# A residual image added to 128 channels: by matmul broadcast and two passes, or by DMA broadcast and one

## The chip, the cores and the metric

The kernel runs on one core of a Trainium2 chip. The metric is the device time of one execution in microseconds (us), so lower is better. The core has five engines that run side by side, each with its own queue of instructions, taken in order: PE (TensorE, matrix products, with PEld for its weight loads), DVE (VectorE), ACT (ScalarE), POOL (GpSimd) and SP (SyncE), which here issues nearly all transfers between DRAM and SBUF. Products land in PSUM[...]. Everything is float32.

## The reference, cut to what matters

Four layers follow each other on an image of 256 × 256 points with 128 channels. Only the last is touched. It normalises the image by groups of channels, runs two kinds of convolution with shifted residuals, and adds the result to its input:

```
def c1(t):  # 9 taps along W, 128 channels to one
    return conv(t, w1) + b1
def c2(t):  # centre tap alone: a 128 x 128 product for each point
    return einsum('bhwc,cd->bhwd', t, w2[0, 4]) + b2
t = relu(c1(x))
y = concat([x[:, :1], x[:, 1:] + t[:, :-1]], axis=1)
u = relu(c1(y))
z = u + roll(y, 1, axis=1)       # with its last rows rearranged
v = relu(c2(z))
p = concat([z[:, :, :1], z[:, :, 1:] + v[:, :, :-1]], axis=2)
r = relu(c2(p))
q = r + roll(p, 1, axis=2)       # with its last columns rearranged
x = x + q
```

Here the inner x is the normalised one, (x - m) * r. Since c1 yields one channel, t and u are images of one number for each point, the same for all channels. So z is the normalised x, shifted by one row, plus an image e that is the sum of u and the shifted t. With the norm written out, z = r3 * x + k0 + e, where r3 and k0 = -m * r3 are one number per channel.

## The kernel before, in words

Channels are the partitions. The stage works on slices of 8 image rows (R = 8, 2048 points, NR = 32 slices), in a loop over s from 0 to 33 (L1419), and on blocks of 16 rows (two slices) for the one-channel images. Within `tc.manual_schedule()` each engine takes its instructions in the order in which the code writes them, so the text of the loop sets the order of the work.

The images take a detour through DRAM. `taps` (L1221) multiplies a slice of x with the nine taps on PE and stores the sums in sD. `load_block` (L1251) reads a block's shifted taps back, with the image spread over 128 partitions; `sum_taps` (L1260), `image_u` (L1276) and `image_e` (L1287) form t, u and e on DVE. t goes through tD (`keep_t`, `load_t`), and e is stored in eD, rows of NP = 264 with margins. In the loop, slices with even s run `sum_taps` and `image_u` of a block at their end, and slices with odd s `image_e`.

e must then reach all 128 channels. `load_e` (L1298) reads the two slices of a block into four partition groups of a small tile `p9_er`, four DMAs a block. `broadcast_rows` (L855) spreads a slice over the partitions with four products of PE with a column of `sel`, into two PSUM tiles of the pool psX. `start_z` (L1307) has ACT write r3 * x + k0 into the tile `p9_z` (two pieces, of 1 and 7 rows), and `finish_z` (L1321) has DVE add the spread e from PSUM, in two halves.

From z on, `p_half` (L1337) takes half a slice: `product9` (L1328) forms w2c times z on PE, and DVE's pass at L1340 turns it into p, reading the product in PSUM and z in SBUF. A constant per channel, `kcol[:, 0:1]`, brings in the bias. `residual` (L1344) adds shifted p to q's start on POOL, reading two tiles in SBUF; q's start is x plus a constant, written by ACT (L1430). `q_half` (L1350) does for r what p_half does for v. The products of p and q share a PSUM pool psM of two buffers, so a product waits until DVE has read the one before the last.

In slice s the order is: on PE the product of z(s), the spread of e(s+1), the product of p(s-1), the taps of slice s+6, and the transposes of q(s-2); on DVE two passes for p(s), two for z(s+1), four for q(s-1) and the image's passes; on POOL the residual of s as soon as p(s) is complete; on SP the load of x(s+8), t or e of a block, the stores of taps, and the output of slice s-2.

`emit` (L1362) transposes q in 16 blocks of 128 points and stores the slice with point k * 128 + p in partition p, which makes a run of 512 bytes for each point.

Of the kernel before, what the change touches and what calls it, by code (L numbers as in the profile page):

```python
# [8 lines left out]
F32 = mybir.dt.float32  # L9
AF = mybir.ActivationFunctionType  # L10
ALU = mybir.AluOpType
# [4 lines left out]
P = 128  # L16
N = 256
D = 128
T = N * N
SC = 2048  # L20
NSC = T // SC
CK = 512
# [5 lines left out]
TAPS = 9  # L28
# [3 lines left out]
def kernel(ctx: ExitStack, tc: tile.TileContext, a: dict, out: bass.AP):  # L32
    nc = tc.nc
    x_tok = a["x"].rearrange("b i j d -> (b i j) d")
    out_tok = out.rearrange("b i j d -> (b i j) d")
# [26 lines left out]
    NP = N + 8  # L62
# [5 lines left out]
    eD = dram.tile([1, N * NP], F32, name="eD")  # L68
# [140 lines left out]
    with tc.tile_pool(name="x0", bufs=1) as xres, tc.tile_pool(name="p0", bufs=3) as sb:  # L209
# [18 lines left out]
        with tc.tile_pool(name="f0", bufs=1) as fsb, tc.tile_pool(name="f0ps", bufs=1, space=PSUM) as ps:  # L228
            cen = fsb.tile([P, P], F32, name="f0_c")
            nc.vector.tensor_scalar(cen, ident, -1.0 / D, None, ALU.add)  # L230
            wa = fsb.tile([P, 4 * D + NH], F32, name="f0_a")
            nc.vector.tensor_scalar(wa, w0, ln_w, None, ALU.mult)
            wb = fsb.tile([P, 4 * D + NH], F32, name="f0_b")
            nc.vector.tensor_scalar(wb, w0, ln_b, None, ALU.mult)
            for lo, hi in ((0, 4 * D), (4 * D, 4 * D + NH)):
                pc = ps.tile([P, hi - lo], F32, name="f0_pc", tag=f"f0_pc{lo}")
                nc.tensor.matmul(pc, lhsT=cen, rhs=wa[:, lo:hi], start=True, stop=True)
                nc.vector.tensor_copy(w0c[:, lo:hi], pc)
            pq = ps.tile([P, 3], F32, name="f0_pq")
            for j, i in enumerate((0, 1, 3)):  # L240
                nc.tensor.matmul(pq[:, j : j + 1], lhsT=w0[:, i * D : (i + 1) * D], rhs=ln_b, start=True, stop=True)
            nc.vector.tensor_copy(cqkg, pq)
            pv = ps.tile([P, D], F32, name="f0_pv")
            nc.tensor.matmul(pv, lhsT=ones, rhs=wb[:, 2 * D : 3 * D], start=True, stop=True)
            for k in range(4):
                nc.vector.tensor_copy(cv[:, k, :], pv)

            w2c_ = const.tile([P, 6, D], F32, name="w2c_")
            wa2 = fsb.tile([P, 6, D], F32, name="f0_a2")
            nc.vector.tensor_scalar(wa2[:, 0:5, :], w2[:, 0:5, :], lniw, None, ALU.mult)  # L250
            nc.vector.tensor_scalar(wa2[:, 5, :], w2[:, 5, :], lnow, None, ALU.mult)
            for lo, hi in ((0, 4), (4, 6)):
                pc = ps.tile([P, (hi - lo) * D], F32, name="f0_pc2", tag=f"f0_pc2{lo}")
                nc.tensor.matmul(
                    pc, lhsT=cen, rhs=wa2[:, lo:hi, :].rearrange("p w d -> p (w d)"), start=True, stop=True
                )
                nc.vector.tensor_copy(w2c_[:, lo:hi, :].rearrange("p w d -> p (w d)"), pc)
            pb2 = ps.tile([P, 6], F32, name="f0_pb2", tag="f0_pb2")
            for i in range(6):
                nc.tensor.matmul(  # L260
                    pb2[:, i : i + 1], lhsT=w2[:, i, :], rhs=lnib if i < 5 else lnob, start=True, stop=True
                )
            nc.vector.tensor_tensor(b2w, b2w, pb2, ALU.add)

            pb2 = ps.tile([P, TAPS + 1], F32, name="f0_ps", tag="f0_pb2")
            nc.tensor.matmul(pb2[:, :TAPS], lhsT=ones, rhs=w1[:, :TAPS], start=True, stop=True)
            nc.vector.tensor_copy(wsum, pb2[:, :TAPS])
            pk = pb2[:, TAPS : TAPS + 1]
            nc.tensor.matmul(pk, lhsT=w2c, rhs=b2, start=True, stop=True)
            nc.vector.tensor_scalar(kcol[:, 0:1], b2, -1.0, None, ALU.mult)  # L270
            nc.vector.scalar_tensor_tensor(kcol[:, 1:2], pk, -1.0, b2, ALU.mult, ALU.subtract)
            nc.vector.scalar_tensor_tensor(kcol[:, 2:3], b2, 2.0, pk, ALU.mult, ALU.add)
            pt_ = ps.tile([P, NH], F32, name="f0_pt")
            nc.tensor.matmul(pt_, lhsT=ones, rhs=wb[:, 4 * D :], start=True, stop=True)
            nc.vector.tensor_copy(ctri, pt_)
# [923 lines left out]

    R = 8
    NR = N // R
    H = R // 2
# [4 lines left out]
    with tc.tile_pool(name="p9", bufs=2) as sb, tc.tile_pool(name="p9psM", bufs=2, space=PSUM) as psM, tc.tile_pool(  # L1209
# [1 line left out]
    ) as psX, tc.manual_schedule():  # L1211
        x3r = x3T.rearrange("d (h w) -> d h w", w=N)
        xs, zs, pbs, qs, blocks = {}, {}, {}, {}, {}
        ers = [sb.tile([P, CK], F32, name=f"p9_er{i}", bufs=1) for i in range(2)]

        def load9(s):
            if s < NR:
# [77 lines left out]
                nc.sync.dma_start(image_rows(eD, N - 2, 1), e[P - 8 : P, :])  # L1295
                nc.sync.dma_start(image_rows(eD, N - 1, 1), k["t"][P - 8 : P, 4 : 4 + BW])

        def load_e(b):  # L1298

            e_chunks = eD.rearrange("o (s c h w) -> c (o s) h w", c=4, h=2, w=NP)  # L1300
            for c in range(4):
                nc.sync.dma_start(
                    ers[b % 2][32 * c : 32 * c + 2, :].rearrange("s (h w) -> s h w", h=2),
                    e_chunks[c, 2 * b : 2 * b + 2, :, 4 : 4 + N],
                )

        def start_z(s):  # L1307

            zs[s] = sb.tile([P, R, N], F32, name="p9_z", bufs=3)

            def take(lo, hi, src):
                nc.scalar.activation(zs[s][:, lo:hi, :], src, AF.Identity, bias=k0, scale=r3)

            take(0, 1, xs[s - 1][:, R - 1 : R, :] if s else xe[:, 1:2, :])
            if s + 1 < NR:
                take(1, R, xs[s][:, 0 : R - 1, :])
            else:
                take(1, R - 2, xs[s][:, 0 : R - 3, :])
                take(R - 2, R, xs[s][:, R - 2 : R, :])

        def finish_z(s):  # L1321
            eb = broadcast_rows(psX, ers[s // 2 % 2], s % 2, "p9_eb")
            zf = zs[s].rearrange("p h w -> p (h w)")
            for h in range(2):
                hs = slice(h * H2, (h + 1) * H2)
                nc.vector.tensor_tensor(zf[:, hs], eb[h], zf[:, hs], ALU.add)

        def product9(src, h):  # L1328
            pm = psM.tile([P, H, N], F32, name="p9_pm")
            for c in range(2):  # L1330
                r = h * H + 2 * c
                nc.tensor.matmul(  # L1332
                    pm[:, 2 * c : 2 * c + 2, :], lhsT=w2c, rhs=src[:, r : r + 2, :], start=True, stop=True
                )
            return pm

        def p_half(s, h):  # L1337
            rows_ = slice(h * H, (h + 1) * H)
            pm = product9(zs[s], h)
            nc.vector.scalar_tensor_tensor(  # L1340
                pbs[s][:, rows_, 1:N], pm[:, :, 0 : N - 1], kcol[:, 0:1], zs[s][:, rows_, 1:N], ALU.max, ALU.add
            )

        def residual(s):  # L1344
# [17 lines left out]
        def emit(s):  # L1362
            qf = qs.pop(s).rearrange("p h w -> p (h w)")
            ot = sb.tile([P, SC // P, D], F32, name="p9_o")
            for h in range(2):
                pt = psX.tile([P, 2 * H, D], F32, name="p9_pt", tag="x")
                for k in range(2 * H):
                    b = h * 2 * H + k
                    nc.tensor.transpose(pt[:, k, :], qf[:, b * P : (b + 1) * P], ident)  # L1369
                nc.scalar.copy(ot[:, h * 2 * H : (h + 1) * 2 * H, :], pt)  # L1370
            nc.sync.dma_start(
                out_tok[s * SC : (s + 1) * SC, :].rearrange("(k p) d -> p k d", p=P), ot
            )

        xe = sb.tile([P, 2, N], F32, name="p9_xe", bufs=1)
        nc.sync.dma_start(xe, x3r[:, N - 2 : N, :])
        for s in range(4):
            load9(s)
        for er in ers:
            nc.gpsimd.memset(er, 0.0)  # L1380
        S0 = sb.tile([P, TAPS, 2 * BW + 8], F32, name="p9_S")
        nc.vector.memset(S0, 0.0)

# [8 lines left out]
        taps(xe, N - 2, 1)  # L1392
        for s in range(2):
            taps(xs[s], s * R, 4)
        start_z(0)
        load_taps(S0, N - 1, 1, BW, BW + 4, P - 8)
        blocks[-1] = dict(St=S0)
        load_block(0)
# [3 lines left out]
        def image(b):  # L1402
            sum_taps(b)
            keep_t(b)
            load_t(b)
            image_u(b)
            image_e(b)
            load_e(b)

        image(0)  # L1410
        for s in range(2, 4):
            taps(xs[s], s * R, 4)
        for s in range(4, 6):
            load9(s)
        finish_z(0)
        load_block(1)
        for s in range(6, 8):
            load9(s)
        for s in range(NR + 2):  # L1419
            load9(s + 8)  # L1420
            b = s // 2 + 2
            if s % 2 == 1 and 2 < b < NB:
                load_t(b)
            if s % 2 == 0 and 3 < b <= NB:
                load_e(b - 1)
            if s < NR:
                pbs[s] = sb.tile([P, R, N], F32, name="p9_pb")
                nc.scalar.activation(pbs[s][:, :, 0:1], zs[s][:, :, 0:1], AF.Identity, bias=kcol[:, 0:1])
                qs[s] = sb.tile([P, R, N], F32, name="p9_q", bufs=3)
                nc.scalar.activation(qs[s], xs[s], AF.Identity, bias=kcol[:, 2:3])  # L1430
                if s + 1 < NR:
                    start_z(s + 1)
                p_half(s, 0)
                p_half(s, 1)
                del xs[s]
            if s + 1 < NR:
                finish_z(s + 1)
            if 0 < s <= NR:
                q_half(s - 1, 0)
                q_half(s - 1, 1)  # L1440
# [207 lines left out]
```

## Time and profile before

| | |
|---|---|
| time, median of 3 runs | 3525.54 us (3513.11 to 3529.35) |
| span of the profiled execution | 3502.3 us |
| last stage (layer 3), in that span | about 3078 to 3502 us |
| busy over the whole span | PE 89%, DVE 66%, ACT 56%, POOL 46% |
| DVE's p passes, L1340, 128x1020 | 64 of 1276 ns |
| DVE's z passes, L1326, 128x1024 | 64 of 1219 ns |
| DVE's q passes, L1354, 128x1016, and their tails, L1357 | 64 of 1270 and of 216 ns |
| POOL's residual, L1346, 128x2024 | 32 of 4505 ns |
| ACT's z pieces, L1312, from 3150 to 3450 us | 1874 and 594 ns |
| ACT's copies of the transposes, L1370, same stretch | 1016 ns |

A row of the profile's groups names a line of the code, the engine and the operation, the tiles (out<-in), the shape, how many there were and the mean time of one, and then how long the engine stood idle just before them and who released it. A timeline row gives start, duration, engine, line and tiles, and merges neighbours of one kind (x8). A float32 product of 512 columns stands as two records. The rows of stretches give, for each stretch, the busy time of every engine and the share of time that the DMA engines were moving packets.

### The profile page before, as it was taken

The page shows a single profiled execution, that of the slowest core. Times are in us where ns is not written, and L with a number is a line of the kernel's source. Part 1 is how long each engine was busy: PE and PEld are TensorE (multiplying, and loading weights), DVE is VectorE, ACT ScalarE, POOL GpSimd, SP SyncE. Part 2 cuts the span into 40 slices and gives each one's busy share as a digit, 9 for nine tenths or more (in the row PEclk, how much of TensorE's full clock was granted, in tenths as well). Part 3 has the DMA queues.
Part 4 walks back from the last instruction along what each step waited for, and adds up shares of the span by engine and source line. Part 5 has one row for each costly group of instructions (what it writes and reads, how often), then busy time and mean ns, then how long its engine had stood idle before and what let it go on. Part 6 is the DMA issues. An engine that isn't in the chain of part 4 may idle for free. (4 is left out here: it accounts for less than half of the span.)

```text
span 3502.3 us, 52445 instructions
## 1 busy us (share of the span) xinstructions
PE 3131.9 (89%) x20260; PEld 1652.7 (47%) x20260; DVE 2316.9 (66%) x2637; ACT 1962.3 (56%) x2198; POOL 1604.9 (46%) x821
## 2 busy tenths in 40 slices
PE   3576999999999999966597899999999999859998
PEld 3523555555555555521432344444899533314444
DVE  4624888888888888852398454544555677647776
ACT  3564777777777777733243454443444466535665
POOL 4002777777777777731487000000555354414443
PEclk7787999999999999989798999999999999979999
DMA  9983333333333333349599686865999798846764
GB/s 334 325 316 114 102 120 115 106 122 115 105 122 112 108 122 111 110 161 392 168 337 351 233 309 229 299 255 206 345 349 351 297 335 303 291 171 193 206 198 136
DMA packets 309867, 759.49 MB, mean 217 GB/s; under 512 B 77627, under 2 KB 148957, under 8 KB 259437
## 3 DMA queue, kind: packets, MB, share of 16 engines
q1 hardware_dynamic: 298749, 746.43, 60.5%
q0 software_dynamic: 10864, 9.65, 0.9%
q8 instruction: 162, 2.65, 0.3%
q14 instruction: 92, 0.75, 0.1%
HBM read 468.28 MB, written 287.66 MB: 216 GB/s over the span
## 5 line engine op out<-in xcount | busy, mean ns | idle before, releaser
L489 DVE TENSOR_TENSOR p_e<-p_S,triT 128x1024 f32<-128x1024 f32 x512 | 609.4, 1212 | 144.5 <-PE p_S L479 144.5
L499 POOL TENSOR_TENSOR p_es<-p_e 128x1024 f32<-128x1024 f32 x256 | 602.9, 2365 | 125.8 <-issue 67.5
L497 ACT ACTIVATE p_e<-p_e,mbT 128x1024 f32<-128x1024 f32 x512 | 551.8, 1137 | 61.4 <-DVE p_e L489 59.6
L946 PE MATMUL p_pm<-p_zn,wf 128*128 128x512 f32 x1040 | 450.4, 595 | 1.4 <-DVE p_zn L963 1.4
L464 PE MATMUL p_mm<-p_xn,wf 128*128 128x512 f32 x768 | 407.6, 614 | 9.3 <-POOL p_xn L437 9.3
L437 POOL TENSOR_TENSOR p_xn<-p_xn,p_rs 128x1024 f32<-128x1024 f32 x64 | 153.5, 2398 | 451.4 <-DMA p_x<-xT 260.4
L946 PEld LDWEIGHTS p_pm<-p_zn,wf 128*128 128x128 f32 x1040 | 197.7, 191 | 254.9 <-issue 248.1
L479 PE MATMUL p_S<-p_q,p_k 32*128 32x256 f32 x4096 | 295.4, 400 | 5.0 <-DVE p_e L489 5.0
L479 PEld LDWEIGHTS p_S<-p_q,p_k 32*128 32x128 f32 x4096 | 185.8, 184 | 161.5 <-PE p_mm L455 91.7
L1346 POOL TENSOR_TENSOR p_q<-p_q,p_pb 128x2024 f32<-128x2024 f32 x32 | 144.2, 4505 | 249.6 <-DVE p_pb L1340 249.6
L1606 PE MATMUL tp_z<-p_B,tp_at 128*128 128x256 f32 x1024 | 250.3, 387 | 2.1 <-DMA p_B<-bD 1.8
L512 PE MATMUL p_o<-p_e,p_v 128*32 128x256 f32 x4096 | 247.6, 382 | 0.0
L1011 POOL DMA_DIRECT2D rs__18021<-rs2D x4 | 2.1, 518 | 532.1 <-PE p_pm L946 532.1
L1054 POOL TENSOR_TENSOR k<-k,p_sq 128x512 f32<-128x512 f32 x128 | 162.9, 1273 | 135.2 <-ACT p_sq L1052 135.2
L1163 POOL TENSOR_TENSOR p_x<-p_x,p_g 128x2048 f32<-128x2048 f32 x30 | 136.2, 4540 | 177.8 <-DVE p_g L1150 146.9
L1606 PEld LDWEIGHTS tp_z<-p_B,tp_at 128*128 128x128 f32 x1024 | 185.3, 191 | 24.4 <-issue 2.2
L464 PEld LDWEIGHTS p_mm<-p_xn,wf 128*128 128x128 f32 x768 | 126.4, 191 | 114.1 <-issue 89.7
L1053 DVE TENSOR_TENSOR k<-tp_z,k 128x512 f32<-128x512 f32 x128 | 88.5, 691 | 128.5 <-ACT p_sq L1052 128.5
L512 PEld LDWEIGHTS p_o<-p_e,p_v 128*32 128x32 f32 x4096 | 120.0, 109 | 109.3 <-ACT p_g L470 41.5
L979 DVE SCALAR_TENSOR_TENSOR p_b<-p_pm,b2w,p_b 128x1024 f32<-128x1024 f32 x64 | 82.2, 1284 | 125.4 <-PE p_pm L946 111.0
L455 PEld LDWEIGHTS p_mm<-wf,p_xn 128*128 128x128 f32 x1024 | 135.3, 192 | 62.3 <-issue 61.1
L1050 ACT COPY p_K<-tp_z 128x512 f32<-128x512 f32 x128 | 75.1, 586 | 159.6 <-PE tp_z L1606 159.6
(353 smaller groups left out, 5902.5 us busy)
## 6 DMA issues: line engine op xcount, KB each, us to landing
p_x<-x2T SPq DMA_DIRECT2D x64, 1024.0 KB
p_x<-x1T SPq DMA_DIRECT2D x48, 1024.0 KB
p_x<-in_x_dram SPq DMA_DIRECT2D x32, 1024.0 KB
p_x<-xT SPq DMA_DIRECT2D x64, 512.0 KB
p_rs<-rsD SPq DMA_DIRECT2D x64, 512.0 KB
p_rb<-rzD SPq DMA_DIRECT2D x256, 128.0 KB
x1T<-p_x SPq DMA_DIRECT2D x64, 512.0 KB
aD<-p_a SPq DMA_DIRECT2D x32, 1024.0 KB
```

The source lines that it names most:

```text
L437: nc.gpsimd.tensor_tensor(xn, xn, t["rs"], ALU.mult)
L464: nc.tensor.matmul(pm, lhsT=w, rhs=t["xn"][:, cs_], start=True, stop=True)
L479: nc.tensor.matmul(Ss[h // 2][:, h % 2, u, :], lhsT=t["k"][hp, r * N + u * P : r * N + (u + 1) * P], rhs=t["q"][hp, r * N : (r + 1) * N], ...
L489: nc.vector.tensor_tensor(e[:, :, 2 * p : 2 * p + 2, :].rearrange("p u h n -> p h u n"), Ss[p], triT[:, 2 * p : 2 * p + 2, :, :], ALU.add,)
L497: nc.scalar.activation(e[:, u, :, :], e[:, u, :, :], AF.Exp, bias=mbT[:, u, i : i + 1])
L499: nc.gpsimd.tensor_tensor(es, e[:, 0, :, :], e[:, 1, :, :], ALU.add)
L512: nc.tensor.matmul(t["o"][hp, r % 2, :], lhsT=t["v"][:, r * 2 + u, hp], rhs=e[:, u, h, :], start=(u == 0), stop=(u == 1),)
L946: nc.tensor.matmul(pm[:, c, :], lhsT=wf2[:, i, :], rhs=zns[s][:, k * CK : (k + 1) * CK], start=True, stop=True)
L1054: nc.gpsimd.tensor_tensor(k2, k2, sq, ALU.add)
L1163: nc.gpsimd.tensor_tensor(xs7[s], xs7[s], gts[s], ALU.add)
L1346: nc.gpsimd.tensor_tensor(q[:, :, 1 : N - 2], q[:, :, 1 : N - 2], pb[:, :, 0 : N - 3], ALU.add)
L1606: nc.tensor.matmul(pz[:, t, :], lhsT=at[:, u, t * P : (t + 1) * P], rhs=Bc[:, u, :], start=(u == 0), stop=(u == 1))
```

## The change

Three things change in the last stage.

- e goes to the channels by DMA. `spread_e` reads a slice of eD, margins included, into every partition of z's own tile, which grows to rows of 264; `load_e`, `p9_er`, and PE's spread go away. It is issued two slices ahead of the slice that uses it.
- z is then made in place by DVE alone: `make_z` computes r3 * x + e in one pass over 7 rows and one over 1 row (the shift by one row makes two sources). ACT's `start_z` goes away. The shift k0 is no longer in z, so it moves to the constants in `kcol`, which are now worked out after the norm is known.
- `emit` transposes every 16th point instead of 128 neighbours, so that partition p ends up with 16 neighbouring points, and stores runs of 8 KB instead of 512 bytes.

The aim is to take work from PE and ACT and to make the output's packets larger.

```diff
-        def load_e(b):
-            e_chunks = eD.rearrange("o (s c h w) -> c (o s) h w", c=4, h=2, w=NP)
-            for c in range(4):
+        def spread_e(s):
+            if s < NR:
+                zs[s] = sb.tile([P, R, NP], F32, name="p9_z", bufs=3)
                 nc.sync.dma_start(
-                    ers[b % 2][32 * c : 32 * c + 2, :].rearrange("s (h w) -> s h w", h=2),
-                    e_chunks[c, 2 * b : 2 * b + 2, :, 4 : 4 + N],
-                )
-        def start_z(s):
-            zs[s] = sb.tile([P, R, N], F32, name="p9_z", bufs=3)
-            def take(lo, hi, src):
-                nc.scalar.activation(zs[s][:, lo:hi, :], src, AF.Identity, bias=k0, scale=r3)
-            take(0, 1, xs[s - 1][:, R - 1 : R, :] if s else xe[:, 1:2, :])
+                    zs[s].rearrange("p h w -> p (h w)"),
+                    eD[:, s * R * NP : (s + 1) * R * NP].to_broadcast([P, R * NP]),
+                )
+        def make_z(s):
+            def add(lo, hi, src):
+                z = zs[s][:, lo:hi, 4 : 4 + N]
+                nc.vector.scalar_tensor_tensor(z, src, r3, z, ALU.mult, ALU.add)
+            if s >= NR:
+                return
             if s + 1 < NR:
-                take(1, R, xs[s][:, 0 : R - 1, :])
+                add(1, R, xs[s][:, 0 : R - 1, :])
             else:
...
-        def finish_z(s):
-            eb = broadcast_rows(psX, ers[s // 2 % 2], s % 2, "p9_eb")
-            zf = zs[s].rearrange("p h w -> p (h w)")
-            for h in range(2):
-                hs = slice(h * H2, (h + 1) * H2)
-                nc.vector.tensor_tensor(zf[:, hs], eb[h], zf[:, hs], ALU.add)
+            add(0, 1, xs[s - 1][:, R - 1 : R, :] if s else xe[:, 1:2, :])
...
         def emit(s):
+            qk = qf.rearrange("c (p k) -> c k p", k=SC // P)
...
-                    nc.tensor.transpose(pt[:, k, :], qf[:, b * P : (b + 1) * P], ident)
+                    nc.tensor.transpose(pt[:, k, :], qk[:, h * 2 * H + k, :], ident)
...
-                out_tok[s * SC : (s + 1) * SC, :].rearrange("(k p) d -> p k d", p=P), ot
+                out_tok[s * SC : (s + 1) * SC, :].rearrange("(p k) d -> p k d", p=P), ot
...
+        pk = psX.tile([P, 2, CK], F32, name="p9_pk", tag="x")
+        nc.tensor.matmul(pk[:, 0, 0:1], lhsT=w2c, rhs=k0, start=True, stop=True)
+        nc.vector.tensor_tensor(kcol[:, 1:2], pk[:, 0, 0:1], b2, ALU.add)
+        nc.vector.tensor_scalar(kcol[:, 0:1], kcol[:, 1:2], -1.0, None, ALU.mult)
+        nc.vector.tensor_tensor(kcol[:, 2:3], kcol[:, 1:2], k0, ALU.add)
+        nc.tensor.matmul(pk[:, 1, 0:1], lhsT=w2c, rhs=kcol[:, 2:3], start=True, stop=True)
...
         for s in range(NR + 2):
...
-            if s % 2 == 0 and 3 < b <= NB:
-                load_e(b - 1)
+            if s:
+                spread_e(s + 2)
             if s < NR:
                 pbs[s] = sb.tile([P, R, N], F32, name="p9_pb")
...
-                if s + 1 < NR:
-                    start_z(s + 1)
                 p_half(s, 0)
                 p_half(s, 1)
-            if s + 1 < NR:
-                finish_z(s + 1)
+            make_z(s + 1)
```

## The prediction

> **What bounds the kernel now.** All edits lie in the last stage (layer 3), so I read that stage alone: first the busy times by stretch, for the engine that sets its pace.
>
> ```profile
> core 0: us, PE busy (x) PEld busy (x) DVE busy (x) ACT busy (x) POOL busy (x), PEclk, DMA share, GB/s
> 3111.00:3163.00 52.00, 38.92 (x136) 14.97 (x136) 32.89 (x46) 23.47 (x26) 14.58 (x9) 0.85 0.55 171
> 3163.00:3442.00 279.00, 271.83 (x1144) 124.99 (x1144) 217.99 (x289) 170.34 (x190) 116.83 (x72) 0.98 0.68 195
> ```
>
> From 3163 to 3442 us PE is busy 97% of the time, DVE 78%, ACT 61%, POOL 42%, DMA 68%. Next the timeline of one slice (a slice is 8 image rows; 32 pass through the loop):
>
> ```profile
> 3301.96 3.60 PE L1332 MATMUL p_pm<-p_z,w2c 128*128 128x512 f32 x8
> ...
> 3304.73 2.46 DVE L1340 SCALAR_TENSOR_TENSOR p_pb<-p_pm,kcol,p_z 128x1020 f32<-128x1020 f32 x2
> ...
> 3305.49 1.14 PE L860 MATMUL p_eb<-p_er,sel 32*128 32x512 f32 x8
> ...
> 3306.56 3.70 PE L1332 MATMUL p_pm<-p_pb,w2c 128*128 128x512 f32 x8
> ...
> 3307.36 4.52 POOL L1346 TENSOR_TENSOR p_q<-p_q,p_pb 128x2024 f32<-128x2024 f32 x1 [6.47 <-DVE p_pb L1340]
> ...
> 3307.60 2.36 DVE L1326 TENSOR_TENSOR p_z<-p_eb,p_z 128x1024 f32<-128x1024 f32 x2 [0.40 <-ACT p_z L1312]
> ...
> 3310.19 1.07 PE L1225 MATMUL p_pp<-p_x,w1f 128*32 128x512 f32 x8
> ...
> 3313.00 3.60 PE L1332 MATMUL p_pm<-p_z,w2c 128*128 128x512 f32 x8
> ```
>
> PE runs without a gap: product of z from 3301.96, spread of e 1.07 us, product of p 3.63, taps 1.00, transposes 1.81, and the next slice starts 11.04 us later. POOL's residual starts 0.17 us after the second DVE pass over p ends at 3307.19, and runs beside DVE's z. The starts of the 32 slices span 3111.7 to 3477.4 us: three ramp intervals sum to 44.0, the next 23 to 271.7 (11.8 each), the last five to 50.1.
>
> Then I looked for what a new DVE instruction with two SBUF inputs would meet, since it will stand exactly beside that POOL pass. The ramp's timeline has one such case:
>
> ```profile
> 3119.01 4.52 POOL L1346 TENSOR_TENSOR p_q<-p_q,p_pb 128x2024 f32<-128x2024 f32 x1 [37.03 <-DVE p_pb L1340]
> ...
> 3121.04 1.35 DVE L1264 TENSOR_REDUCE p_acc<-p_S 128x74 f32<-128x666 f32 x1
> ...
> 3122.43 1.17 DVE L1266 SCALAR_TENSOR_TENSOR p_t<-p_acc,b,p_in 128x41 f32<-128x41 f32 x1
> 3123.48 0.23 POOL L1347 TENSOR_TENSOR p_q<-p_q,p_pb 128x16 f32<-128x16 f32 x1
> ```
>
> The one-input reduction runs at its usual length beside POOL. The two-input one takes 1.17 us where its median over 17 is 0.264, and ends at 3123.60, just after POOL's at 3123.53: it stood until POOL was through. Last, the weight loads of transposes, for contiguous data (L1369) and for every second element (L1595):
>
> ```profile
> L1369 PEld LDWEIGHTS p_pt<-ident,p_q x512: 137/141/146, 3153.9 to 3493.2; 128*128 128x128 f32 x171
> ...
> L1595 PEld LDWEIGHTS tp_a<-ident,p_A x512: 194/205/231, 2452.4 to 2741.1; 128*128 128x128 f32 x171
> ```
>
> **What the Trainium skill says.** SBUF — State Buffer, section "Who interferes with whom": a VectorE instruction with two SBUF inputs contends with a GpSimd instruction that reads SBUF, the first to issue keeps the shared port for its whole length, and the other fully blocks. The trace agrees in the case above (0.264 to 1.17 us); z's present pass reads PSUM and SBUF and keeps its 1.22 us beside POOL, as the page would have it. The same page, section "Door 1: The DMA port swizzle", note on cachelines: each access that crosses to a new 16-byte line pays, and at least two hits to a line are needed to hide it. The trace is stricter: two hits to a line already cost 0.205 against 0.141 us. DMA: Bandwidth & Descriptors, "Issuing engines are not separate DMA queues": all transfers share 16 DMA engines. Here nearly all are on one queue, and the issues show their order: e's rows, asked for at 3321.64, reach PE at 3328.24, behind the block of taps, the output and x asked for before them.
>
> **The change part by part, per slice.**
>
> 1. PE loses the spread of e, 1.07 us (3305.49 to 3306.56). Nothing else hides it: a gain on the path while PE is the bound. 11.04 − 1.07 = 9.97.
>
> 2. ACT loses start_z, 1.87 + 0.59 = 2.46 us (means of L1312). ACT is 61% busy and only delays the first half of z by 0.40; worth nothing by itself.
>
> 3. The stepped transposes load 128 elements 64 bytes apart. Contiguous data touches 32 lines of 16 bytes in a load, step 2 touches 64 and takes 0.064 us more: 2 ns a line. Step 16 touches 128: 0.26 us for each load, if only its fixed part overlaps the one before, against a spacing of 0.109 between transposes now. Upper bound 16 × 0.15 = 2.4 us; lower bound 16 × 0.008 = 0.13 (with step 2, transposes start 0.117 apart). I take 1.7, nearer the upper end: lines are what grows, but step 2's records also hold some waiting for the matmul in front. PE: 11.7 per slice.
>
> 4. The output leaves in 8 KB packets: the trace's packet records give 31 ns for 512 bytes (2048 packets over 16 engines: 3.97 us) and 309 ns for 8 KB (128: 2.5 us). Saves 1.4 us of DMA, off the path now at a 68% share.
>
> 5. e arrives as 1.08 MB by broadcast instead of 8 KB: 128 packets of 8448 bytes, 2.6 us at the same rate. DMA per slice becomes 0.68 × 11.8 = 8.0 − 1.4 + 2.6 = 9.2 us: below any pace predicted here. But latency: e written at 3314.11 was on PE at 3328.24, 14.1 us. The change adds 2.6 − 1.4: some 15.3 us. The queue behind it on SP is the tD write and the taps; they need nothing sooner than a slice later.
>
> 6. DVE: two passes of z, 2.36 us, become one over 7 rows and one over 1 row, both from x and e in SBUF. L939, of the same form, takes 2.345 us for 2048: 7/8 gives 2.06, and 0.34 for 256. The sum of 2.4 is no loss. What it meets is: the 7-row pass follows DVE's second pass over p at once, takes the port, and POOL's residual, ready 0.17 us later, waits. When the 7-row pass ends, POOL was issued first, takes the port for 4.5 us, and DVE's 1-row pass stands. From the end of p to z complete: 2.06 + 0.1 + 4.5 + 0.15 = 6.8 us, where it is 2.77 now. If the port stays with DVE for the second pass: 2.4.
>
> 7. Behind the blocked pass on DVE are the q passes (2.71) and, on alternate slices, the image's sums (3.37: 3301.45 to 3304.82). PE waits for both z of the next slice and the two PSUM buffers of p_pm, which the q passes free. Count from the end of p: z at 6.8, first q pass and its tail 8.3, first half of the next product (1.8) 10.1, first p pass 11.5, second half of the product 11.9, second p pass 13.3. With the image: q ends at 9.5, image 12.9, two p passes 15.4. Mean 14.35 us a slice, with DVE the bound, PE at 11.7 hidden.
>
> 8. The constants (six tiny DVE operations, two PE products) fall into DVE's 14.0 us wait for the first taps. The first slices take e about 2 us later, since the broadcast is longer.
>
> Sum: 23 intervals × (14.35 − 11.8) = 58; five × (13.3 − 10.0) = 16; ramp 8 (two port waits, less than 4.5 each, or late e); tail, two slower sets of transposes, 3. Together +85 on 3525.5: **3610 us**.
>
> **The rivals.**
>
> A. DVE keeps the port for both passes, and strided loads cost little. PE 9.97 + 0.13 = 10.1; DVE's two slices hold 2 × (2.46 + 2.4 + 2.71) + 3.37 + 0.2 = 18.7, and about 2 of waits for the port in the image's two-input sums: 10.4 a slice. 23 × −1.4 − 5 + 3: 3492 us. For it: the spread of e was pure PE time. Against: the port trace, and e's 15.3 us must fit between e's pass at the end of one slice and z's use of it after the p passes of the slice after next, one slice and 2.5 us: 13 at this pace.
>
> B. DVE keeps the port, but the transposes cost their 1.7: PE sets 11.7 to 12, and late e lets POOL go first in some odd slices. 23 × 0.2 + 5 × 0.6 + 6: near 3540 us.
>
> **How the numbers follow.** Main case 0.60, because the one port case in the trace is clean and the order of issue favours POOL at the second pass; but no row shows who wins when one engine's next instruction and the other's waiting one meet. B 0.24, A 0.16. The range runs from A's upper edge through B to the main case with 30 us above it (a port wait at each image sum): 3512 to 3640; outside lie most of A and a sliver above. Faster by over 0.5% (under 3508) is A, 0.17; within 0.5% (3508 to 3543) two thirds of B, 0.15; the rest slower.
>
> **What would show it.** Right: the 1-row z pass at some 4.8 us instead of 0.34, or POOL's residual at 6.5 instead of 4.5; z-passes ahead of PE's idle time; weight loads of p_pt near 0.3 us; slices 13 and 15 us apart in turn. Wrong: the 1-row pass at 0.34 us while POOL waits (then A or B, told apart by the spacing of the transposes, 0.11 or 0.21), or POOL's pass slowed only in part. If DVE waits for p_z's DMA instead, latency was the bound.

## The result, and the profile after

| | before | after |
|---|---|---|
| median of 6 runs | 3519.32 us (3499.5 to 3529.35) | 3615.1 us (3609.18 to 3640.16) |
| ratio, 95% interval | | 1.0292 [1.0249, 1.0336] |
| span of the profiled execution | 3502.3 us | 3607.4 us |
| last stage, from the norm's factor to the end | 421.6 us | 532.4 us |
| mean interval of the 23 slices after the ramp | 11.8 us | 14.9 us |

The changed kernel is slower by 2.9%. The predicted 3610 us stood within 0.2% of it. But several of the prediction's sizes were wrong, in opposite directions, so the sum alone doesn't show the reasoning right; the steps have to be looked at one by one.

First the busy times from 3180 to 3440 us, the middle of the stage, before and then after (busy time and number of records of each engine; the last three columns are the granted clock of PE, the DMA engines' busy share, and GB/s).

```profile
3180.00:3440.00 260.00, 253.35 (x1079) 117.46 (x1072) 203.89 (x272) 161.16 (x180) 108.60 (x69) 0.99 0.69 197
```

```profile
3180.00:3440.00 260.00, 207.20 (x709) 97.48 (x708) 233.96 (x210) 86.06 (x104) 118.78 (x52) 0.88 0.70 236
```

The bound has moved. PE falls from 97% to 80%, DVE rises from 78% to 90%, though DVE finished fewer instructions (210 against 272): its instructions got longer. ACT lost its share of z. DMA carries more bytes at the same busy share. And the clock fell from 0.99 to 0.88. The groups of the new kernel, from 3150 to 3560 us, show which DVE instruction grew (mean ns of one is the number after the busy time):

```profile
L1335 POOL TENSOR_TENSOR p_q<-p_q,p_pb 128x2024 f32<-128x2024 f32 x28 | 173.4, 6191 | 239.4 <-DVE p_pb L1329 239.4
L1320 PE MATMUL p_pm<-p_z,w2c 128*128 128x512 f32 x216 | 146.4, 841 | 75.3 <-DVE p_q L1346 62.9 <-issue 12.4
L1305 DVE SCALAR_TENSOR_TENSOR p_z<-p_x,gn_rstd,p_z 128x256 f32<-128x256 f32 x27 | 127.8, 4732 | 0.0
L1305 DVE SCALAR_TENSOR_TENSOR p_z<-p_x,gn_rstd,p_z 128x1792 f32<-128x1792 f32 x28 | 58.1, 2075 | 0.0
L1358 PEld LDWEIGHTS p_pt<-ident,p_q 128*128 128x128 f32 x432 | 51.1, 196 | 21.6 <-issue 21.6
```

The pass over one row takes 4732 ns, more than twice the pass over seven (2075), and POOL's residual 6191 instead of 4506. The 1-row pass alone takes 0.48 us (it does so in two experiments below); one that takes ten times as long is not working, it is waiting inside the instruction. No wait row names this, since those rows come from semaphores. PE's idle time before the product of z is put down to DVE's q pass (L1346), the last link behind the blocked row. Two slices in the order of time (start, duration; neighbours merged):

```profile
3327.31 6.73 DVE L1305 SCALAR_TENSOR_TENSOR p_z<-p_x,gn_rstd,p_z 128x1792 f32<-128x1792 f32 x2
...
3327.57 6.19 POOL L1335 TENSOR_TENSOR p_q<-p_q,p_pb 128x2024 f32<-128x2024 f32 x1 [8.00 <-DVE p_pb L1329]
...
3333.97 1.26 DVE L1343 SCALAR_TENSOR_TENSOR p_q<-p_pm,kcol,p_q 128x1016 f32<-128x1016 f32 x1
...
3335.28 1.26 DVE L1343 SCALAR_TENSOR_TENSOR p_q<-p_pm,kcol,p_q 128x1016 f32<-128x1016 f32 x1
...
3335.41 6.68 PE L1320 MATMUL p_pm<-p_z,w2c 128*128 128x512 f32 x8 [2.90 <-DVE p_q L1346]
...
3341.93 3.60 PE L1320 MATMUL p_pm<-p_pb,w2c 128*128 128x512 f32 x8
...
3343.33 6.74 DVE L1305 SCALAR_TENSOR_TENSOR p_z<-p_x,gn_rstd,p_z 128x1792 f32<-128x1792 f32 x2
```

This is the predicted order: both z passes last 6.73 us together, POOL starts its records 0.26 us after them, inside the time that the 7-row pass holds the port, and lasts to 3333.76; DVE's 1-row pass ends at 3334.04, and its next pass starts 0.21 us after POOL is through. New is the product of z: eight records took 3.60 us before and take 6.68 here, with no wait among them. The busy times of 3.4 us stretches show why (PEclk is the third number from the end):

```profile
3328.00:3331.40 3.40, 3.40 (x20) 1.50 (x19) 3.40 (x2) 0.69 (x1) 3.40 (x1) 1.00 1.05 368
3331.40:3334.80 3.40, 1.11 (x10) 0.92 (x9) 3.40 (x2) 2.60 (x4) 2.90 (x3) 0.97 0.99 330
3334.80:3338.20 3.40, 2.79 (x4) 1.24 (x5) 3.36 (x6) 1.73 (x2) 0.00 (x0) 0.50 0.57 241
3338.20:3341.60 3.40, 3.40 (x6) 1.39 (x5) 2.74 (x7) 0.00 (x0) 0.00 (x0) 0.52 0.30 89
3341.60:3345.00 3.40, 3.40 (x10) 1.41 (x8) 2.87 (x2) 0.00 (x0) 1.42 (x1) 1.00 0.99 306
```

PE is idle for 2.90 us up to 3335.41, and the clock is 0.5 for the two stretches from 3334.8 on. From the ramp to the 13th interval some of PE's gaps do this and some don't: the slices stand 14.9 and then 13.0 or 14.7 us apart. From the 14th on every second gap does it for one stretch and every other for two, and the slices stand 16.0 and 14.7 apart. Between the first products of the fourth and of the last slice the clock was low for 110 us, in the kernel before for 10.

The length of the gap alone doesn't decide it. A gap of 2.91 us from 3186.54 left the clock full, and one of 2.45 from 3201.91 halved it (two stretches each, around the gap and behind it):

```profile
3187.80:3191.20 3.40, 1.75 (x4) 0.87 (x5) 3.40 (x6) 2.40 (x3) 0.54 (x2) 1.00 0.99 411
3191.20:3194.60 3.40, 1.95 (x5) 0.57 (x3) 3.19 (x8) 0.00 (x0) 0.00 (x0) 1.00 0.36 124
3201.50:3204.90 3.40, 0.95 (x6) 0.52 (x5) 3.40 (x4) 3.31 (x4) 1.75 (x3) 1.00 0.64 268
3204.90:3208.30 3.40, 3.40 (x6) 1.33 (x5) 1.43 (x4) 0.57 (x2) 0.00 (x0) 0.50 0.14 27
```

In this trace the low stretches of the clock from 3150 us on all begin on one fixed grid of 3.41 us. PE had been busy for at most 40% of the grid step before each fall, and for at least 43% of each step after which the full clock stayed. So it matters how a gap falls on the grid. And 16.0 and 14.7 us together make nine grid steps (30.7 us), so from the 14th interval on each pair of gaps falls on it alike.

### The profile page after: what moved, and what is told of

It reads as the page before. It is cut to its first block, busy times and chain, and to the rows that moved or that the text cites. A ratio compares the mean times of both kernels' runs of the same rounds, so it can differ in the third digit from the quotient of the medians.

```text
span 3607.4 us, 51809 instructions
## 1 busy us (share of the span) xinstructions
PE 3146.4 (87%) x20006; PEld 1664.8 (46%) x20006; DVE 2443.5 (68%) x2640; ACT 1892.0 (52%) x2133; POOL 1660.4 (46%) x819
## 4 chain that ended last, share of the span: by engine, by line
PE 37%; DMA 5%; DVE 5%; issue 4%; ACT 1%; SPq 0%; POOL 0%; ACTq 0%; DVEq 0%; POOLq 0%
PE p_pm L941 12%; PE tp_z L1598 6%; PE p_pm L1093 6%; PE p_pm L1320 5%; DMA x2T<-p_x 2%; DVE p_z L1305 2%; PE tp_a L1587 2%; PE p_st L898 1%; PE p_pg L805 1%; PE p_rz L855 1%; DVE p_pb L1329 1%; PE p_rk L855 1%; DVE p_q L1343 1%; PE p_pz L813 0%; PE p_pt L1358 0%
## 5 line engine op out<-in xcount | busy, mean ns | idle before, releaser
L1335 POOL TENSOR_TENSOR p_q<-p_q,p_pb 128x2024 f32<-128x2024 f32 x32 | 194.1, 6066 | 320.0 <-DVE p_pb L1329 320.0
L1320 PE MATMUL p_pm<-p_z,w2c 128*128 128x512 f32 x256 | 177.4, 858 | 113.7 <-DVE p_q L1346 67.3
L1305 DVE SCALAR_TENSOR_TENSOR p_z<-p_x,gn_rstd,p_z 128x256 f32<-128x256 f32 (+2 forms) x64 | 206.4, 3265 | 13.3 <-DMA p_z<-eD 13.3
```

Source lines behind the costliest of these rows:

```text
L1305: nc.vector.scalar_tensor_tensor(z, src, r3, z, ALU.mult, ALU.add)
L1320: nc.tensor.matmul(pm[:, 2 * c : 2 * c + 2, :], lhsT=w2c, rhs=src[:, r : r + 2, src.shape[2] - N >> 1 :][:, :, 0:N], start=True, stop=True,)
L1335: nc.gpsimd.tensor_tensor(q[:, :, 1 : N - 2], q[:, :, 1 : N - 2], pb[:, :, 0 : N - 3], ALU.add)
```

## The experiments

Ratios are to the kernel before, run beside each of these kernels, so they compare better across experiments than the times do.

**The port's order.** The first experiment separates the blocked row from everything else: the 1-row pass moves to the place between DVE's two passes over p, where POOL's residual isn't ready yet.

```diff
-        def make_z(s):
+        def make_z(s, part=(0, 1)):
...
                 p_half(s, 0)
+                make_z(s + 1, (0,))
                 p_half(s, 1)
-            make_z(s + 1)
+                make_z(s + 1, (1,))
```

> The changed kernel, with z's 1-row pass moved from behind the 7-row pass to between the two passes for p; the work is the same. Port theory (POOL's residual takes the shared SBUF port when the 7-row pass lets go of it, and the next two-input pass stands for 4.5 us): no two-input pass follows the 7-row pass any more, so the 1-row pass takes 0.3 to 0.5 us instead of 4.7, POOL's residual still stands about 2 us at its start, slices are 10.3 to 10.8 us apart, and the kernel takes 3480 to 3505 us, under the kernel before. Rival (the megabyte of e per slice, its latency of some 15 us, or the stepped transposes set the pace): the passes may change, but slices stay at 14 us or more and the time above 3590 us, with DVE waiting for p_z's DMA.

Measured: 3530.67 us, ratio 1.0041 [1.0019, 1.0063]. The 1-row pass takes 0.48 us, and nearly all of the loss is gone. That shows where the loss sat. It doesn't give the gain that was expected beyond it: slices alternate between 9.9 us, as PE's sum without the spread has it, and 11 to 18. What holds the longer ones is in the timeline of one:

```profile
3314.16 1.66 DVE L1285 TENSOR_TENSOR p_e<-p_u,p_t 128x33 f32<-128x33 f32 x1 [0.16 <-DMA p_t<-tD]
...
3315.84 0.32 SPq L1287 DMA_DIRECT2D eD<-p_e  x1
...
3331.89 0.48 DVE L1305 SCALAR_TENSOR_TENSOR p_z<-p_x,gn_rstd,p_z 128x256 f32<-128x256 f32 x1 [3.37 <-DMA p_z<-eD]
```

e's pass, again with two inputs in SBUF, takes 1.66 us beside POOL, where it takes 0.18 in the kernel after. e is stored at 3315.84 and first used by the spread at 3331.89, 16.05 us later, and DVE has waited 3.37 us for it. The broadcast itself is issued only at 3321.40, behind the stores of the taps, the block of taps, the output and x. In the kernel after this wait is hidden: its slices are so long that e is there.

The second takes POOL away instead: the kernel after without the residual's large pass (L1335), so most of p isn't added to q.

> The changed kernel without POOL's large residual pass (it leaves out adding p to q for most columns, so the work of POOL is not done). Port theory: nobody competes for the port, the 1-row pass takes about 0.3 to 0.5 us where it stands, slices are about 10.3 us apart, 3475 to 3500 us. Rival (DMA of e or transposes): still above 3590 us.

Measured: 3507.28, ratio 0.9961 [0.9939, 0.9983], a little above the range expected; for most of the stage slices of 10.0 to 10.8 us stand beside slices of 11.7 to 13.9. Without a rival for the port the same two DVE passes in the same place take 2.08 and 0.48 us, and the next wait shows:

```profile
DVE p_z L1305 <- DMA p_z<-eD: 33.4, 11, 4.5
```

(total us from 3180 to 3480 us, times, the longest). It is the largest of DVE's waits there, so what is missing from the forecast went at least in part to it. The third swaps DVE's two z passes, so that the longer one comes second:

```diff
         def make_z(s):
...
+            add(0, 1, xs[s - 1][:, R - 1 : R, :] if s else xe[:, 1:2, :])
             if s + 1 < NR:
                 add(1, R, xs[s][:, 0 : R - 1, :])
...
-            add(0, 1, xs[s - 1][:, R - 1 : R, :] if s else xe[:, 1:2, :])
```

> The changed kernel with the two passes for z in the other order, the 1-row pass first and the 7-row pass behind it. Port theory (whoever stands in second place behind the first release is blocked, whatever its size): the 1-row pass takes 0.5 us, POOL's residual is held back for a few tenths only (4.5 to 5 us in the record instead of 6.2), the 7-row pass takes 2.1 + 4.4 = 6.5 us; z is complete as late as before, so the time is within 20 us of the changed kernel. Rival (the 1-row pass is slow for a reason of its own, such as its source in another tile): it stays at 4.7 us and the 7-row pass at 2.1.

Measured: 3616.4 us in one run, and in the profile (groups from 3150 to 3560 us):

```profile
L1305 DVE SCALAR_TENSOR_TENSOR p_z<-p_x,gn_rstd,p_z 128x1792 f32<-128x1792 f32 x27 | 170.9, 6330 | 0.0
L1335 POOL TENSOR_TENSOR p_q<-p_q,p_pb 128x2024 f32<-128x2024 f32 x27 | 123.9, 4587 | 237.1 <-DVE p_pb L1329 237.1
L1336 POOL TENSOR_TENSOR p_q<-p_q,p_pb 128x16 f32<-128x16 f32 x27 | 54.2, 2009 | 0.0
L1305 DVE SCALAR_TENSOR_TENSOR p_z<-p_x,gn_rstd,p_z 128x256 f32<-128x256 f32 x27 | 12.8, 475 | 0.0
```

The blocked instruction is now the 7-row pass: 6330 ns, its own 2075 and most of POOL's 4.5 us. When POOL's large pass ends, DVE's waiting pass takes the port, and POOL's tiny second pass (0.23 us in the kernel before) stands 2.0 us for it. So in both orders the port goes over at each instruction's end to the engine that waits, whatever the sizes; the holder's next instruction doesn't keep it.

**The output.** One kernel is the change with the old output, one the kernel before with the new output alone.

```diff
-            qk = qf.rearrange("c (p k) -> c k p", k=SC // P)
...
-                    nc.tensor.transpose(pt[:, k, :], qk[:, h * 2 * H + k, :], ident)
+                    b = h * 2 * H + k
+                    nc.tensor.transpose(pt[:, k, :], qf[:, b * P : (b + 1) * P], ident)
...
-                out_tok[s * SC : (s + 1) * SC, :].rearrange("(p k) d -> p k d", p=P), ot
+                out_tok[s * SC : (s + 1) * SC, :].rearrange("(k p) d -> p k d", p=P), ot
```

> The changed kernel with the output of the kernel before (transposes of neighbours, runs of 512 bytes). Port theory: DVE is the bound, PE and DMA have room, so within 8 us of the changed kernel (3615), the 1-row pass still at 4.7 us. Rival (stepped weight loads cost 1.7 us a slice on the path): faster by some 50 us. Rival (large packets are what keeps it from being slower still): slower by 20 us or more.

Measured: 3631.57, ratio 1.032 [1.0261, 1.0379]; 16 us above the kernel after by medians, where at most 8 was expected. Its four runs (3628.65 to 3636.26) lie within the six of the kernel after, so the difference may be smaller than that, or nothing. The traces show one difference: its slices go to 16.0 and 14.7 apart from the sixth interval on instead of the 14th, and the clock was low for 137 us instead of 110 between the fourth and the last slice. The old output's transposes load their weights in 141 ns instead of 196, and PE's gap is 2.99 us instead of 2.90. Whether this tips the clock was not tested by itself; the kernel with the passes swapped, whose gaps are the same 2.90 us, falls into the slow pattern at the eighth interval, so it may as well be the place of the gaps on the clock's grid.

The opposite edit, the same lines put into the kernel before (there L1369, L1372):

> The kernel before with the new output alone (stepped transposes, runs of 8 KB). The traces give transposes 0.113 us apart instead of 0.109, so PE loses 0.07 us a slice, 2 us in all; the output takes 1.4 us less of the DMA engines, so e's rows arrive sooner where PE waited for them (6.4 us over the steady slices). Expected 0 to 8 us under the kernel before. If stepped loads cost the 1.7 us of the prediction, 50 us above it.

Measured: 3505.95, ratio 0.9965 [0.9943, 0.9987], the one kernel that does all of the work and is faster than both. Its busy times from 3180 to 3440 us:

```profile
3180.00:3440.00 260.00, 259.50 (x1108) 120.51 (x1107) 212.56 (x280) 167.37 (x186) 114.55 (x70) 1.00 0.62 198
```

DMA fell from 0.69 to 0.62 and PE has no gap. From the fifth interval to the 26th its slices stand 11.1 us apart (one 11.2), where before seven took 11.3 to 15.4; from 3180 to 3440 us PE waited 6.4 us for e before and not at all here, and DVE 17.2 us for t before and 9.7 here. The packets take less DMA time, and what queues behind them arrives sooner. The profiled execution is one of the fastest of its kernel (3486.81 us against the median of 3505.95), so not every run can be this even.

**The clock.** If PE's idle gap slows the products, filling the gap must make the kernel faster although PE does more. Two idle products of 512 columns go behind each slice's taps, into a part of that PSUM tile which nobody reads.

```diff
+            for c in range(2 if h0 >= 8 * R and h0 < N - 2 else 0):
+                nc.tensor.matmul(pp[:, 1, :], lhsT=w2c, rhs=x[:, 2 * c : 2 * c + 2, :], start=True, stop=True)
```

> The changed kernel with two more products of 512 columns (1.8 us of PE) in each slice's taps from slice 8 on, whose results nobody reads: PE is idle for 2.9 us a slice in the changed kernel, and in its later slices the product of z after that gap takes 5.4 to 6.7 us instead of 3.6 at a granted clock of 0.5, with slices 16.0 and 14.7 us apart instead of 14.9 and 13.0. Clock theory: the shorter gap keeps the clock up, slices go back to 14.9 and 13.0 or less, and the kernel is 15 to 35 us faster although PE does more. Rival (PE's lower clock follows from power or is hidden behind DVE): no change, or slower.

Measured: 3594.92, ratio 1.0237 [1.02, 1.0273]: 20 us below the kernel after by medians. The two intervals of the ratio just overlap (1.0249 to 1.0336 there), but all four runs (3587.08 to 3601.84) lie below all six of the kernel after (from 3609.18). Its product of z (3150 to 3560 us):

```profile
L1322 PE MATMUL p_pm<-p_z,w2c 128*128 128x512 f32 x225 | 113.0, 648 | 37.3 <-issue 20.8 <-DVE p_q L1348 16.5
```

648 ns a record instead of 841, the clock low for 32 us instead of 110 between the fourth and the last slice, slices at 14.9 (now and then 15.9) and 13.0 nearly to the end. PE's gaps are 2.1 us at most up to 3490; about there the taps end, and the filler with them.

**What stands behind the port.** Since the row moved between the p passes ran into late e, the next kernel also issues every second broadcast earlier: right behind the stores of the taps of the slice before, ahead of the block of taps, the output and x.

```diff
-            if s:
+            if s % 2 or s == 2:
                 spread_e(s + 2)
...
+            if s > 2 and s % 2:
+                spread_e(s + 3)
```

> The kernel with the 1-row pass between the passes for p, in which DVE still waits for p_z's DMA (31 us in all, e's write to its use 16 us), with every second broadcast of e issued right after the taps' stores of the slice before, ahead of the block of taps, the output and x. Latency theory: e arrives some 7 to 9 us after its write instead of 16, DVE no longer waits for it, slices come to 9.9 to 10.6 us each, and the kernel takes 3470 to 3495 us, under the kernel before and under the kernel before with the new output alone. Rival (PE, DVE or the port set the 11 to 18 us of the longer slices): stays near 3530.

Measured: 3521.47, ratio 1.0031 [1.0013, 1.0048]; the interval overlaps that of the kernel without it, and the gain that was expected did not come. DVE's waits for transfers from 3180 to 3440 us:

```profile
DVE p_acc L1259 <- DMA p_S<-sD: 14.5, 8, 2.7
DVE p_e L1285 <- DMA p_t<-tD: 13.6, 8, 2.8
...
DVE p_z L1305 <- DMA p_z<-eD: 3.7, 4, 1.1
```

The wait for e fell from 30.1 us to 3.7, but with nearly all transfers on one queue, what moved forward moved others back: DVE now waits for the block of taps and for t. The last kernel takes POOL's large residual out of this one as well (most of p isn't added to q), so that POOL hardly competes for the port any more.

> The kernel with the 1-row pass between the passes for p and the early broadcast of e, and without POOL's large residual pass (it leaves out adding p to q for most columns). With neither the port nor e's latency in the way, only PE (10.1 us a slice) and DVE's image passes in alternate slices (some 10.9 us of DVE work) are left. If these two waits are all that separates the change from its gain, slices come to 9.9 and 10 to 11 us and the kernel takes 3470 to 3490 us. If DVE's image passes alone make PE wait and lose its clock, slices with the image stay at 11 to 15 us and the time stays above 3500.

Measured: 3508.0, ratio 0.9981 [0.9958, 1.0004]; the time and the slices of the second outcome named, though DVE's waits are for transfers and not only its own image passes. From 3180 to 3440 us:

```profile
3180.00:3440.00 260.00, 233.75 (x906) 111.55 (x905) 208.10 (x271) 109.03 (x135) 47.88 (x46) 0.97 0.89 298
```

```profile
DVE p_acc L1259 <- DMA p_S<-sD: 14.4, 10, 2.0
DVE p_e L1285 <- DMA p_t<-tD: 12.7, 8, 2.2
DVE p_z L1305 <- DMA p_z<-eD: 5.7, 5, 1.8
```

PE is at 90%, DMA at 0.89. Slices of 9.9 us stand beside slices of 10.7 to 16: DVE waits for the image's transfers (32.8 us in this stretch), its passes over p come late, and PE waits for those (26.2 us). Even with the port and late e out of the way, most of the 1.07 us a slice that PE gained is given back there: the 23 intervals sum to 264.1 us against 271.6 before, where 1.07 each would have saved 24.6. Whether it is the load of the DMA engines or the place in the queue that makes t and the taps late, no run tells.

## Why the prediction was right, step by step

The profiled executions allow an account by parts of the last stage, which grew by 110.8 us (the unchanged stages in front took 5.6 less in this execution; by medians the whole grew by 95.8).

| part | predicted | measured |
|---|---|---|
| up to the first product of z | none in the sum | 4.2 |
| three ramp intervals | 8 | 7.2 |
| 23 intervals | 58 | 71.9 |
| last five intervals | 16 | 26.3 |
| after the start of the last product of z | 3 | 1.2 |

- **The port (steps 6 and 7), right in mechanism and size.** Predicted 2.06 us for the 7-row pass, 4.8 for the 1-row pass, 6.5 for POOL's; measured 2.075, 4.732 and 6.191. (Alone, the 1-row pass was put at 0.34; it takes 0.48.) Slices of 15.4 and 13.3 were worked out; with the clock up they are 14.9 and 13.0. The kernel with the filler gives nearly the share of this alone: its 23 intervals sum to 323.6 us, 52.0 over the 271.6 of before, against a predicted 58 (58.65, rounded down). The Trainium skill (SBUF — State Buffer, "Who interferes with whom") says that the first to issue takes the pair for a whole instruction; all three port experiments agree, and they add what the argument had to guess, who follows at an instruction's end.
- **The stepped transposes (step 3), wrong in size.** Taken at 1.7 us a slice; loads take 196 ns and the transposes start 0.113 us apart instead of 0.109, 16 × 0.004 = 0.07 us, about half of the lower bound of 0.13. The failed sentence is "lines are what grows": step 16 loads no slower than step 2 (205 ns). The error hardly reached the sum, because PE was hidden behind DVE in the main case: only the tail, put at 3 and measured at 1.2, holds some of it. In rival B it would have been most of the effect.
- **PE's clock, missing.** The working gave each product its 3.60 us though it also left PE idle in each slice. The Trainium skill (TensorE: Matmul & The Clock Gate, "What's actually happening") has two states of the clock, half and full, and a fall to half after an idle window of about 3.4 us; the records of these traces have no other value than 0.5 and 1. But the gap in front is 2.90 us, less than such a window, and while the gaps were 2.90 us PE was busy for 15% to 40% of the grid step before each fall, so the clock falls here on less than an idle window. The cost in the 23 intervals is the kernel after less the filled one, 343.6 − 323.6 = 20.0 us, where the slices are otherwise alike. The last five, 76.3 us against the predicted 66.5, stand 16.0 and 14.8 apart at a clock of 0.84 (3505 to 3581 us); the filler hardly reaches them (74.0 us), so that share is argued and not shown.
- **So the sum.** Over the 23 intervals the port came 6 us lower than forecast, and a clock that the forecast lacked added 20. By medians the growth was 95.8 instead of 85, and the forecast started from a median for the kernel before that lay 6 us above the later one (3525.5, 3519.3). That the total agrees within 5 us is luck: the working had the direction, the mechanism and the larger part of the size; what the missing clock cost was largely made up for by the other errors.
- **e's latency (step 5).** 15.3 us predicted, 16.05 in the kernel with the row moved. In the kernel after it was rightly off the path. As the bound of a faster version it was rightly seen in rival A, but too lightly: that version was put at 3492, and the kernel with the port out of the way came to 3530.67.
- **Rivals A and B.** The signs named for them did not come: the 1-row pass behind the 7-row pass never kept its own time beside POOL. Rival A's 3492 was too low even for a kernel in which DVE never loses the port (3507.28).
- **The output's packets (step 4).** Called worth nothing while off the path; alone in the kernel before they are worth 0.35%, since late transfers were on the path in some slices; the mean of 11.8 beside the steady 11.04 could have told.

## What to carry to other kernels

Before a DVE instruction with two SBUF inputs goes beside a POOL pass, look at what follows it: one such instruction delays POOL once, but two in a row let POOL in between, and the second then stands for all of POOL's pass while everything behind it on DVE waits; move the small one to a place where POOL has nothing ready. Work taken from the bound pays only until the next wait: here most of PE's 1.07 us a slice went to waits for transfers, so read what the freed engine will wait for, the clock after its new gaps included.

## What the hardware showed that was not expected

- The shared port goes over in turn at each instruction's end: a pass of 0.48 us stood for 4.73, in the other order a pass of 2.08 for 6.33 and then one of 0.23 for 2.01.
- A weight load of PE in float32 takes 141 ns for 128 neighbouring elements, 205 for every second and 196 for every 16th; the step from 8 to 64 bytes cost nothing more here.
- Gaps of 2.45 to 2.9 us can halve PE's clock for one or two steps of 3.41 us, and others of the same length leave it full. In the kernel after, the clock fell when PE had been busy for at most 40% of a step of the clock's own grid, and not when it had been busy for 43% or more. More work for PE, 48 idle products, made the kernel 20 us faster by medians.
